# Softmax denominators from one product per head: GpSimd adds the node blocks first, and the product moves behind the value sums

## The chip, the cores and the metric

The kernel runs on one core of a Trainium2 chip. The metric is the device time of one execution in microseconds (us); lower is better. Each kernel was run several times, and times are medians of these runs. All runs told here were of the fast state; the verdict on a change is "faster" or "slower" only beyond 2%. Ratios are computed as the mean time of one kernel's fast runs over that of the other's fast runs of the same rounds, which is not quite the ratio of the medians quoted.

In profile lines PE is TensorE (PEld its weight loads), DVE is VectorE, ACT is ScalarE, POOL is GpSimd, and L722 is line 722 of the kernel.

## The reference, cut to what matters

Two layers on 64 graphs of 256 nodes: a graph-attention layer with a feed-forward block, then an attention layer with 8 heads of 32 features whose values depend on the adjacency (0 or 1 here).

```python
scores = jnp.einsum('bhid,bhjd->bhij', q, k) / np.sqrt(dh)
attn = jax.nn.softmax(scores, axis=-1)
for r in range(Wv.shape[0]):
    v_r = (src @ Wv[r] + bv[r]).reshape(Bb, Nn, h, dh).transpose(0, 2, 1, 3)
    mask = (adj_matrix == r)[:, None]
    out = out + jnp.einsum('bhij,bhjd->bhid', attn * mask, v_r)
```

The kernel works with the transposed exponentials e[j, i] (nodes j on the 128 partitions, so two node blocks). The denominator of row i is a sum over all j, that is over partitions and over both blocks; TensorE forms it as a product with a block of ones.

## The kernel before

A turn of the main loop takes the attention of one pair of graphs together with the first layer's stages of two later pairs, so that TensorE always has something to do. There are 32 turns with attention. A turn has four quads: two graphs, each with two groups of four heads. In what follows "step" is the time from one turn to the next, "the last step" the one from the last turn but one to the last, and "the tail" the time from the last turn's first value product (vp) to the end.

```python
def weighted(u, b, m, q, k_, aT):               # scores, exponentials, masked product
    ps = [bank(f"sp{n}_{a}") for a in range(HPB)]
    ...                                          # sp: scores of four heads
    e = work.tile([P, HPB, NB * N], F32, tag="e", name=f"e{n}")
    ea = work.tile([P, HPB, NB * N], F32, tag="ea", name=f"ea{n}")
    for a in range(HPB):
        nc.scalar.activation(e[:, a, :], ps[a], AF.Exp, scale=isd)
    for a in range(0, HPB, 2):                   # two instructions, two heads each
        nc.vector.tensor_tensor(ea[:, a:a + 2, :], e[:, a:a + 2, :],
                                ab[:, None, :].to_broadcast([P, 2, NB * N]), ALU.mult)
    return e, ea

def applied(b, m, v, e, ea, po, zo):             # zo: denominators, po: value sums
    terms = [(zo, lambda h, j: ones, e), (po, ..., e), (po, ..., ea)]
    ...                                          # per term: two node blocks x four heads

def divided(u, b, po, zo, oT):
    nc.vector.reciprocal(rz, zo)
    nc.gpsimd.tensor_add(low, low, rz)
    nc.vector.tensor_tensor(oT[...], po..., rz..., ALU.mult)

def normed(u, l, y):                             # layer norm; rs is on GpSimd
    ...
    nc.gpsimd.tensor_tensor(rs, ve, mhalf, ALU.pow)
    ...

def affine(u, l, xn, g, b):                      # res, L644 and L645
    nc.gpsimd.tensor_mul(r, xn, g...)
    nc.gpsimd.tensor_add(r, r, b...)

# in a turn, TensorE runs in this order (cut):
hT = to_features(Y["y"], ...)                    # h2T
second_sums(x_)                                  # ygp; then yg = normed(...), affine(...)
q, k_ = queries_keys(y_, hT)
h1hT = to_features(X["y"], ...)                  # h1T: transposes of yg
v = values(y_, hT)                               # vp
e = {0: weighted(y_, *quads[0], q, k_, aT)}
h1 = hidden(...)                                 # h1p, first half
e[1] = weighted(y_, *quads[1], q, k_, aT)
apply_(0)
e[2] = weighted(y_, *quads[2], q, k_, aT)
apply_(1)
e[3] = weighted(y_, *quads[3], q, k_, aT)
hidden(...)                                      # h1p, second half
early(z)                                         # transposes of a later pair
apply_(2)
apply_(3)
...
res = affine(y_, 3, yn, rg4, rb4)                # last thing of the turn, then the store
```

zo and po have one PSUM bank each. TensorE's order is the program's; the other engines are ordered by the framework's scheduler.

## Time and profile before

| | before |
|---|---|
| time (median of 3 runs) | 3486.24 us |
| TensorE busy | 97% of the span |
| one turn | 105.80 us |
| zo in a turn | 64 instructions (4 quads of 16) |
| GpSimd busy | 28% |

TensorE is the engine to look at: a turn is as long as TensorE takes for it, plus the waits of TensorE. The prediction shows the busy shares, the chain in order of time and the timelines on which it rests. Two groups by line (columns: busy us, mean ns of one instruction, idle time before them):

```profile
L710 DVE TENSOR_TENSOR ea<-e,aT 128x1024 f32<-128x1024 f32 x256 | 317.9, 1283 | 272.7 <-ACT e L708 272.7
L722 PE MATMUL zo<-e,ones 128*32 128x256 f32 x2048 | 137.1, 385 | 3.0 <-DVE rz L728 3.0
```

And TensorE's timeline at the start of a turn:

```profile
1822.05 3.60 PE L674 MATMUL kp<-h2T,wk 128*128 128x512 f32 x8
1827.04 1.65 PE L540 MATMUL h1T17p<-ident,yg 128*128 128x128 f32 x8 [1.39 <-DVE yg L637]
```

TensorE waits 1.39 us for yg and then takes 1.65 in place of 1.04 us for the eight transposes, because yg comes in four pieces: VectorE's four instructions for it begin 0.32 us apart (1826.48 to 1827.45), and the second to fourth transposes begin 0.23 to 0.32 apart (1827.04 to 1827.91), the last three 0.11.

### The profile page before, as it was taken

Reading aid. Unit: us, or ns where it says so; the run is one execution under the profiler, and the core shown is the slowest. Engines: PE = TensorE matmul, PEld = TensorE weight load, DVE = VectorE, ACT = ScalarE, POOL = GpSimd, SP = SyncE. Lnnn points to the kernel's source line nnn. Section 1 sums busy time; section 2 is a strip of 40 time slices with the busy share of each in tenths; the row PEclk is TensorE's granted clock in tenths of the full one; section 3 lists DMA queues with packets and bytes.
Section 4 is the critical chain, followed back from the end, with each engine's and each line's share of the span. In section 5 each row is a group of like instructions: output and inputs, shape, how many; then the busy total and the mean of one; then the engine's idle time right before and its main releaser. Section 6 shows DMA issues by size and latency. Waiting matters only on the chain.

```text
span 3486.0 us, 45212 instructions
## 1 busy us (share of the span) xinstructions
PE 3368.1 (97%) x18970; PEld 2201.8 (63%) x18970; DVE 1688.8 (48%) x3479; ACT 1080.4 (31%) x1920; POOL 984.6 (28%) x844
## 2 busy tenths in 40 slices
PE   5899999999999999999999999999999999999997
PEld 3566666666665666665666666666656665656664
DVE  2545455445454444554454554454544445544544
ACT  1323333323323323333333333233233233333322
POOL 1233232332222332322332323322223323223312
PEclk7999999999999999999999999999999999999998
DMA  4000000000000000000000000000000000000000
GB/s 119 19 13 19 7 19 19 13 19 10 16 19 19 13 19 7 19 19 19 13 19 7 19 19 13 19 12 14 19 19 13 19 7 19 19 19 7 7 1 14
DMA packets 62465, 61.04 MB, mean 18 GB/s; under 512 B 7216, under 2 KB 61616, under 8 KB 62256
## 3 DMA queue, kind: packets, MB, share of 16 engines
q1 hardware_dynamic: 33792, 33.56, 3.0%
q0 software_dynamic: 16896, 16.78, 2.1%
q10 hardware_dynamic: 11568, 7.76, 0.8%
q8 instruction: 151, 2.47, 0.3%
q14 instruction: 58, 0.48, 0.0%
HBM read 41.31 MB, written 16.78 MB: 17 GB/s over the span
## 4 chain that ended last, share of the span: by engine, by line
PE 86%; POOL 6%; DVE 6%; issue 1%; ACTq 1%; DMA 0%; ACT 0%; POOLq 0%; DVEq 0%
PE h1p L655 26%; PE yfp L617 25%; PE vp L686 6%; PE po L722 6%; PE sp L702 4%; PE zo L722 4%; PE hpp L606 3%; PE yop L617 3%; PE xpp L568 3%; POOL res L644 2%; POOL res L645 2%; POOL rs L633 2%; DVE yf L637 1%; DVE h2T L544 1%; PE rows L578 1%
## 5 line engine op out<-in xcount | busy, mean ns | idle before, releaser
L655 PE MATMUL h1p<-h1T,wf 128*128 128x512 f32 x1024 | 458.1, 600 | 0.1
L710 DVE TENSOR_TENSOR ea<-e,aT 128x1024 f32<-128x1024 f32 x256 | 317.9, 1283 | 272.7 <-ACT e L708 272.7
L655 PE MATMUL h1p<-h3T,w 128*128 128x512 f32 x1024 | 446.7, 594 | 1.4 <-DVE h3T L544 1.4
L617 PE MATMUL yfp<-wf,h 128*128 128x256 f32 x2048 | 447.3, 379 | 0.0
L617 PE MATMUL yfp<-w,h 128*128 128x256 f32 x2048 | 447.3, 379 | 0.0
L617 PEld LDWEIGHTS yfp<-w,h 128*128 128x128 f32 x2048 | 386.8, 190 | 52.2 <-issue 1.0
L617 PEld LDWEIGHTS yfp<-wf,h 128*128 128x128 f32 x2048 | 386.7, 190 | 51.3
L708 ACT ACTIVATE e<-sp 128x512 f32<-128x512 f32 x512 | 264.3, 603 | 444.9 <-PE sp L702 444.9
L655 PEld LDWEIGHTS h1p<-h3T,w 128*128 128x128 f32 x1024 | 195.0, 191 | 234.4 <-issue 229.5
L729 POOL TENSOR_TENSOR low<-low,rz 128x512 f32<-128x512 f32 x64 | 81.2, 1269 | 917.2 <-DVE rz L728 917.2
L655 PEld LDWEIGHTS h1p<-h1T,wf 128*128 128x128 f32 x1024 | 190.1, 190 | 236.9 <-issue 218.2
L587 DVE SCALAR_TENSOR_TENSOR s<-s 128x512 f32<-128x512 f32 x128 | 90.2, 706 | 443.3 <-ACT s L584 442.0
L645 POOL TENSOR_TENSOR res<-res,rb 128x1024 f32<-128x1024 f32 x128 | 301.3, 2354 | 10.0
L620 DVE TENSOR_TENSOR yf<-yfp,res 128x512 f32<-128x512 f32 x128 | 88.5, 692 | 424.6 <-PE yfp L617 423.4
L633 POOL TENSOR_TENSOR rs<-ve,mhalf 128x4 f32<-128x4 f32 x128 | 130.7, 1021 | 457.9 <-DVE ve L632 457.9
L657 ACT ACTIVATE h<-h1p,b 128x512 f32<-128x512 f32 x256 | 175.9, 687 | 251.1 <-PE h1p L655 249.8
L728 DVE RECIPROCAL rz<-zo 128x512 f32<-128x512 f32 x64 | 214.7, 3354 | 67.8 <-PE zo L722 67.8
L657 ACT ACTIVATE h<-h1p,bf 128x512 f32<-128x512 f32 x256 | 177.1, 692 | 216.0 <-PE h1p L655 216.0
L686 PE MATMUL vp<-wv,h2T 128*128 128x512 f32 x512 | 225.0, 592 | 0.0
L676 ACT ACTIVATE q<-qp,bq 128x512 f32<-128x512 f32 x64 | 44.0, 688 | 530.8 <-PE qp L674 530.8
L608 ACT COPY hp<-hpp 128x258 f32<-128x258 f32 x128 | 48.0, 375 | 442.0 <-PE hpp L606 442.0
L644 POOL TENSOR_TENSOR res<-yf,rg 128x1024 f32<-128x1024 f32 x64 | 150.8, 2356 | 95.8 <-DVE yf L637 94.3
(485 smaller groups left out, 4343.4 us busy)
## 6 DMA issues: line engine op xcount, KB each, us to landing
xs<-in_x_dram SPq DMA_DIRECT2D x32, 512.0 KB, 3.8
af<-in_adj_dram POOLq DMA_DIRECT2D x32, 512.0 KB, 4.5
out_dram<-res SPq DMA_DIRECT2D x32, 512.0 KB, 2.9
wf<-in_L_gnn_w_ff_dram ACTq DMA_DIRECT2D x2, 1024.0 KB, 11.4
w<-in_L_gnn_W_dram ACTq DMA_DIRECT2D x2, 1024.0 KB, 9.5
wv<-in_L_gnn_Wv_dram ACTq DMA_DIRECT2D x2, 256.0 KB, 4.5
gw<-in_L_gnn_W_dram ACTq DMA_DIRECT2D x1, 256.0 KB, 4.5
gw2e<-in_L_gnn_W_dram ACTq DMA_DIRECT2D x1, 256.0 KB, 6.9
```

The source lines that it names most:

```text
L617: nc.tensor.matmul(ps[:, i * F:(i + 1) * F], lhs(t, k), rhs(b, k), start=(k == 0), stop=(k == n - 1))
L633: nc.gpsimd.tensor_tensor(rs, ve, mhalf, ALU.pow)
L644: nc.gpsimd.tensor_mul(r, xn, g[:, None, :].to_broadcast([P, T, F]))
L645: nc.gpsimd.tensor_add(r, r, b[:, None, :].to_broadcast([P, T, F]))
L655: nc.tensor.matmul(ps, wi[:, k, f * P:(f + 1) * P], hT[:, k, :], start=(k == 0), stop=(k == KB - 1))
L657: nc.scalar.activation(h1[:, f, :], ps, func, bias=bi[:, f:f + 1])
L686: nc.tensor.matmul(ps, hT[:, k, t * P:(t + 1) * P], wvf[:, k, :], start=(k == 0), stop=(k == KB - 1))
L702: nc.tensor.matmul(ps[a][:, j * N:(j + 1) * N], k_[hp, m, j0:j0 + P], q[hp, m, b * N:(b + 1) * N], start=True, stop=True)
L708: nc.scalar.activation(e[:, a, :], ps[a], AF.Exp, scale=isd)
L710: nc.vector.tensor_tensor(ea[:, a:a + 2, :], e[:, a:a + 2, :], ab[:, None, :].to_broadcast([P, 2, NB * N]), ALU.mult)
L722: nc.tensor.matmul(to[hp, m * N:(m + 1) * N], lhs(m * HPB + a, j), rhs[:, a, j * N:(j + 1) * N], start=(n < 2 and j == 0), stop=(n != 1 an ...
L728: nc.vector.reciprocal(rz, zo)
```

## The change

The intent: TensorE is the bound, and half of the products with ones can go if the two node blocks of e are added first. The add goes to GpSimd, which is idle 72% of the time, and zo goes behind po to give the add time.

```diff
-        return e, ea
+        es = work.tile([P, HPB, N], F32, tag="es", name=f"es{n}")
+        nc.gpsimd.tensor_add(es, e[:, :, 0:N], e[:, :, N:2 * N])
+        return e, ea, es
...
-        terms = [(zo, lambda h, j: ones, e), (po, ..., e), (po, ..., ea)]
...
+        terms = [(j, v[:, b * NB + j, r * F + m * P:r * F + (m + 1) * P], w)
+                 for r, w in ((0, e), (1, ea)) for j in range(NB)]
+        for n, (j, vs, w) in enumerate(terms):
+            for a in range(HPB):
+                hp = slice(a * DH, (a + 1) * DH)
+                nc.tensor.matmul(po[hp, m * N:(m + 1) * N], vs[:, hp], w[:, a, j * N:(j + 1) * N],
+                                 start=(n == 0), stop=(n == len(terms) - 1))
+        for a in range(HPB):
+            nc.tensor.matmul(zo[a * DH:(a + 1) * DH, m * N:(m + 1) * N], ones, es[:, a, :],
+                             start=True, stop=True)
```

More of the change, by code (lines that the diff above doesn't have):

```diff
@@ L711, in weighted, with applied @@
                                     ab[:, None, :].to_broadcast([P, 2, NB * N]), ALU.mult)
-        return e, ea
-    def applied(b, m, v, e, ea, po, zo):
-        terms = [(zo, lambda h, j: ones, e), (po, lambda h, j: v[:, b * NB + j, h * DH:(h + 1) * DH], e),
-                 (po, lambda h, j: v[:, b * NB + j, F + h * DH:F + (h + 1) * DH], ea)]
-        for n, (to, lhs, rhs) in enumerate(terms):
-            for j in range(NB):
-                for a in range(HPB):
-                    hp = slice(a * DH, (a + 1) * DH)
-                    nc.tensor.matmul(to[hp, m * N:(m + 1) * N], lhs(m * HPB + a, j),
-                                     rhs[:, a, j * N:(j + 1) * N],
-                                     start=(n < 2 and j == 0), stop=(n != 1 and j == NB - 1))
+        es = work.tile([P, HPB, N], F32, tag="es", name=f"es{n}")
+        nc.gpsimd.tensor_add(es, e[:, :, 0:N], e[:, :, N:2 * N])
+        return e, ea, es
+    def applied(b, m, v, e, ea, es, po, zo):
+        terms = [(j, v[:, b * NB + j, r * F + m * P:r * F + (m + 1) * P], w)
[8 more added lines that the diff above has]
+                             start=True, stop=True)
     def divided(u, b, po, zo, oT):
```

## The prediction

> **What bounds the kernel now.** I read the page first: busy shares, then the chain that ended last.
>
> ```profile
> PE 3368.1 (97%) x18970; PEld 2201.8 (63%) x18970; DVE 1688.8 (48%) x3479; ACT 1080.4 (31%) x1920; POOL 984.6 (28%) x844
> ...
> PE 86%; POOL 6%; DVE 6%; issue 1%; ACTq 1%; DMA 0%; ACT 0%; POOLq 0%; DVEq 0%
> ```
>
> TensorE has work 97% of the span and carries 86% of the chain, so a product taken away there is time won unless something makes TensorE wait. The busy figure alone does not say what a product costs, because the matmuls overlap: the table of groups gives 379 ns for one, though many run at once. For spacing I read the chain in order of time, in one turn of the loop (columns: start us, length us, what). There are 32 such turns, 105.80 us apart (the pieces of the chain from 1708.69 and from 1814.49 begin alike).
>
> ```profile
> 1843.69 1.08 PE sp L702 x16
> 1844.77 1.00 PE zo L722 x16
> 1845.77 1.73 PE po L722 x32
> 1847.49 1.08 PE sp L702 x16
> 1848.57 1.00 PE zo L722 x16
> 1849.57 1.73 PE po L722 x32
> 1851.30 1.08 PE sp L702 x16
> 1852.37 7.06 PE h1p L655 x16
> 1859.43 0.87 PE aTp L555 x8
> 1860.31 0.87 PE xT18p L540 x8
> 1861.18 1.00 PE zo L722 x16
> 1862.18 1.73 PE po L722 x32
> 1863.91 0.86 PE zo L722 x16
> 1864.77 1.73 PE po L722 x32
> 1866.50 1.92 PE yop L617 x8
> ```
>
> No gap anywhere: here TensorE sets the pace. One quad is sp (scores), zo (denominators, 16 instructions), po (value sums, 32). po runs at 1.73/32 = 54 ns an instruction, and so does the zo that follows a po (0.86/16). A zo that follows other work takes 1.00, so changing over to the column tiles costs 0.14. The scores run one quad ahead: sp at 1843.69 is quad 1's, the zo and po after it are quad 0's. Quad 1's scores end at 1844.77 and its zo starts at 1848.57, the shortest way from scores to use; quads 0, 2 and 3 have h1p (7.06 us) and more in between.
>
> What runs beside quad 1 and after, from the timeline of ScalarE, VectorE and GpSimd:
>
> ```profile
> 1844.78 2.07 ACT L708 ACTIVATE e<-sp 128x512 f32<-128x512 f32 x4 [0.37 <-PE sp L702]
> ...
> 1845.90 2.36 DVE L710 TENSOR_TENSOR ea<-e,aT 128x1024 f32<-128x1024 f32 x2 [5.78 <-ACT e L708]
> ...
> 1856.04 2.85 DVE L710 TENSOR_TENSOR ea<-e,aT 128x1024 f32<-128x1024 f32 x2
> ...
> 1855.41 1.27 POOL L729 TENSOR_TENSOR low<-low,rz 128x512 f32<-128x512 f32 x1 [22.69 <-DVE rz L728]
> ```
>
> The exponentials of quad 1 end at 1846.85, its two masked products ea at 1848.26. GpSimd is idle from 1832.7 to 1855.41. The ea pair of quad 3 takes 2.85 in place of 2.36: it began inside GpSimd's low, which ended at 1856.68.
>
> [...] the 0.49 lost above. It recurs: ea's mean is 1283 ns and its median 1221, and 256 x 0.062 = 16 us is 0.5 in each of 32 turns. It also shows who goes next, in an early turn:
>
> ```profile
> 114.70 1.83 DVE L587 SCALAR_TENSOR_TENSOR s<-s 128x512 f32<-128x512 f32 x1
> 116.45 2.83 DVE L587 SCALAR_TENSOR_TENSOR s<-s 128x512 f32<-128x512 f32 x1
> ...
> 113.63 2.35 POOL L644 TENSOR_TENSOR res<-yf,rg 128x1024 f32<-128x1024 f32 x1 [1.50 <-DVE yf L637]
> 116.06 2.67 POOL L645 TENSOR_TENSOR res<-res,rb 128x1024 f32<-128x1024 f32 x1
> ```
>
> L587 normally takes 0.71 (its group's mean). The first waits out L644 (ends 115.98); L645, waiting from 116.06, then gets in ahead of the second, though VectorE issued the two back to back; the second ends at 119.28, 0.55 after L645. [...]
> [...] an untiled product of the same 256 columns costs 447.3/2048 = 218 ns (group yfp of the page), four column tiles share that time at 54 ns each; and the changeover is the 0.14.
> [...] Here: 2354 ns (L645) against 1221 for the usual ea, both 128x1024, 1.93 times.
>
> **The change, part by part.**
> Removed: per quad, two ones-products per head become one: 8 of 16 zo instructions. 8 x 54 ns = 0.43 us; 128 quads (4 in each of 32 turns): 55.4 us. The changeover of 0.14 stays and moves to po. All of it lies on TensorE's unbroken stretch.
> Added: per quad one GpSimd add, 128x1024 out, two inputs; by L645's row 2.35 us. 128 x 2.35 = 301 us of GpSimd, which goes from 985 to about 1286 us (37%): no bound. Taken beside TensorE, if in time.
> Moved: zo goes behind po, so the reciprocal starts later against the end of the quad. For the second graph: zo end, reciprocal 3.35, then (the built order puts the addition yo in between) 0.65 and oT 0.69, together 4.75; until its user, the second yop, TensorE has the first yop 1.92 and xpp 3.51 = 5.43. It fits by about 0.7. For the first graph h1p and the transposes lie between, 8.8 us.
>
> Now whether es is in time, quad by quad. Quad 0 has h1p between scores and use: in time. Quads 2 and 3: [...] (es 2.35, ea 1.2 each, reciprocal, low 1.27) I get ea and es of quad 3 done 0.6 to 1.3 us before their use. Quad 1 is the tight one. In the new order, from sp at 1843.69: po of quad 0 starts 1844.77, 1.87 long, zo 0.43, sp of quad 2 1.08, so po of quad 1 starts at 1848.15: its e half to 1849.15, the first ea instructions to about 1849.37, po's end 1850.02, then zo.
> es of quad 1 can start at 1846.9 (exponentials ended 1846.85). The first ea ends at 1847.12, the second starts right behind. As in the early turn, I expect [...] es to end at 1849.4, and the second ea, 1.08 after that (1857.76 against 1856.68 in quad 3; the earlier pair's 0.55 is for half the size), at 1850.45. TensorE, which needs the second ea at 1849.37, waits 1.1 us a turn: 32 x 1.1 = 35 us.
> Sum: 3486.2 - 55.4 + 35 = 3466.
>
> **The rivals.**
> (A) The sum above: [...] 3466. For it: the alternation shown. Against: GpSimd would be ahead by some 0.1 us only.
> (B) [...] ea is on time (1848.26), es runs 1848.2 to 1850.55, and zo, due at 1850.02, waits 0.55: 32 x 0.55 = 18 us, 3449. For it: VectorE's second product is issued before the first ends.
> (C) No collision that matters: 3486.2 - 55.4 = 3431. For it: es alone would end at 1849.3, 0.7 before its use. Against: the 0.49 of quad 3, turn after turn.
> (D) GpSimd lateness spreads: low, the load of adj or the second oT come later and TensorE stops at yop or xpp as well, another 0.5 us a turn on top of A: 3482. Slacks of 0.6 to 1.3 speak against it.
> GpSimd as the bound of the whole (37%) is out.
>
> **Range and chances.** I give A 0.52, B 0.27, C 0.15, D 0.06. Mean: 0.52 x 3466 + 0.27 x 3449 + 0.15 x 3431 + 0.06 x 3482 = 3457; I state 3458, between A and B. Range from C to a bad A: 3431 to 3476. Faster by over 2% is below 3416.5; even the full 55 us is only 1.6%, so 0.03. Slower by over 2% (3556) would need over 3.9 us of new waits a turn: 0.01.
>
> **What would show it.** zo's instructions fall from 2048 to 1024 and its group's busy time to about half of 137 us; ea's mean rises above 1283 ns, with one of quad 1's two at about 3.4 us; in the chain, a VectorE piece between the po instructions of quad 1 (A), a GpSimd piece between po and zo (B), or neither (C). The step of 105.80 us a turn should become about 105.2 (A), 104.6 (B) or 104.1 (C). I am wrong if an instruction saved is worth other than 54 ns, if the wait in quad 1 is not there or much longer, or if TensorE waits in a quad that I called safe.

Cut from this text, where marked, are passages on the hardware that no trace of this case shows. The sum came to 3466: 3486.2 - 55.4 (saved) + 35 (32 waits of 1.1 us). The 1.1 is the estimate, from lengths in the traces: es ends at 1849.4 if it goes in behind the first ea (2.35 us, L645's row), and the second ea 1.08 after it, as in quad 3. That es goes in there is taken from one early turn alone, in which L645 began at 116.06 and the second L587 at 116.45. The 0.6 to 1.3 us for quads 2 and 3 are an estimate as well, with the lengths given there laid one after the other over both engines. In rival A the add goes ahead of the second ea, in rival B behind it. The "changeover" is the measured difference of 1.00 and 0.86 us: in the single records the first four zo behind the scores begin 0.32 us after the last four of these (1844.37 and 1844.70) and the next four 0.24 later, in place of 0.22 each. What TensorE does in it was not shown.

## The result, and the profile after

The changed kernel took 3495.82 us (3495.09 to 3496.76, 6 runs) against 3485.89 us before: ratio 1.0029, 95% interval 1.0016 to 1.0042. It is 10 us slower, within 2%, and above the stated range of 3431 to 3476.

The page's busy shares and chain, and the groups that answer to those shown of before:

```profile
PE 3333.4 (95%) x17946; PEld 2172.3 (62%) x17946; DVE 1950.5 (56%) x3479; ACT 1083.9 (31%) x1920; POOL 1358.4 (39%) x972
...
PE 82%; DVE 10%; POOL 6%; issue 1%; ACTq 1%; DMA 0%; ACT 0%; POOLq 0%
...
L710 DVE TENSOR_TENSOR ea<-e,aT 128x1024 f32<-128x1024 f32 x256 | 527.5, 2101 | 162.5 <-ACT e L708 162.5
L713 POOL TENSOR_TENSOR es<-e 128x1024 f32<-128x1024 f32 x128 | 347.5, 2715 | 414.9 <-ACT e L708 414.9
```

The 1024 zo instructions are gone from TensorE (18970 to 17946). VectorE gained 262 us of busy time though it got no new instruction: the mean ea went from 1283 to 2101 ns. VectorE's share of the chain went from 6% to 10%. Now one turn's chain in order of time (start, length, what); it starts, like the one in the prediction, at the scores of quad 1:

```profile
1839.25 1.08 PE sp L702 x16
1840.33 1.17 PE po L723 x17
1841.50 0.02 issue
1841.52 1.02 DVE ea L710
1842.54 0.13 issue
1842.67 3.46 DVE ea L710
1846.12 0.04 issue
1846.17 0.84 PE po L723 x10
1847.01 0.01 PE zo L726 x2
1847.02 0.20 PE po L723 x2
1847.22 0.43 PE zo L726 x6
1847.65 1.08 PE sp L702 x16
```

A second ea of 3.46 us stands between two stretches of po. GpSimd's add, and TensorE at the same place:

```profile
1842.55 2.48 POOL L713 TENSOR_TENSOR es<-e 128x1024 f32<-128x1024 f32 x1 [5.65 <-ACT e L708]
...
1844.52 0.60 PE L723 MATMUL po<-ea,v 128*32 128x256 f32 x4
1846.17 0.84 PE L723 MATMUL po<-ea,v 128*32 128x256 f32 x10 [1.04 <-DVE ea L710]
```

The add starts at 1842.55, 0.12 before the second ea, and ends at 1845.03; that ea ends at 1846.11. At its usual pace TensorE would be done with the four ea instructions of the first line at 1844.52 + 4 x 0.054 = 1844.74; it goes on at 1846.17, 1.43 later (the line's 1.04 counts from the modelled end of the fourth). In the single records po begins four at a time, the four within 0.02 us, and the next four 0.216 us (4 x 0.054) later. The first ea holds only two of the four heads, so these four instructions began two at a time, at 1844.52 and 1844.74, and took two such slots and not one: of the 1.43, TensorE stood still for 1.21 (1846.17 - 1844.74 - 0.216). From the scores of quad 1 to those of quad 3 it takes 1847.65 - 1839.25 = 8.40 us, against 1851.30 - 1843.69 = 7.61 before. Two quads should have saved 0.86, so the wait cost 8.40 - (7.61 - 0.86) = 1.65. Quads 2 and 3 save their 0.86 undisturbed. The turn is thus about 0.1 shorter than before: the trace has 105.70 for 105.79 (measured from the first vp of one turn to that of the next), so that of the saving of 1.73 the wait takes 1.64.

The whole difference of the two traces, by stretches of TensorE's timeline:

| stretch | before | after | difference |
|---|---|---|---|
| start to the first vp | 135.85 | 132.78 | -3.07 |
| 30 steps from turn to turn | 3173.78 | 3172.94 | -0.84 |
| last step | 93.54 | 95.58 | +2.04 |
| last turn's vp to the end | 82.80 | 92.27 | +9.47 |
| span | 3485.97 | 3493.58 | +7.60 |

The first row varies between 131.3 and 136.6 over the fourteen experiments below without regard to their edits, so it is no effect of the change. The 30 steps would be -2.6 but for two steps of 106.11 and 106.99 among the 105.70s, together +1.7. The last two rows are where the loss is: in the last turns no later pair fills TensorE's time. TensorE's timeline there, before:

```profile
3424.18 1.94 PE L722 MATMUL zo<-e,ones 128*32 128x256 f32 x16 [3.02 <-DVE rz L728]
...
3433.74 1.99 PE L617 MATMUL yop<-wo,oT 128*128 128x256 f32 x8 [0.64 <-DVE oT L730]
```

and after:

```profile
3416.49 0.84 PE L723 MATMUL po<-ea,v 128*32 128x256 f32 x10 [2.06 <-DVE ea L710]
...
3431.36 1.94 PE L723 MATMUL po<-e,v 128*32 128x256 f32 x16 [7.36 <-DVE oT L733]
...
3441.95 1.99 PE L617 MATMUL yop<-wo,oT 128*128 128x256 f32 x8 [2.69 <-DVE oT L733]
```

Before, the second graph's zo came first and waited 3.02 us for the reciprocal of the first graph (one bank). Now its po comes first and waits 7.36 us for oT, which comes after that reciprocal, which in turn started only when zo, behind po, was done. The add has a part in it too: po of the last turn's quad 0, which has no h1p before it there, waits 2.06 us for ea. By the view by windows TensorE is busy 59.94 us of this tail and was busy 59.83 of it before, so the 9.47 us are all waiting.

### The profile page after: what moved, and what is told of

Read it like the earlier page. It is cut to its first block, busy times and chain, and to the rows that moved or that the text cites. A ratio compares the mean times of both kernels' runs of the same rounds, so it can differ in the third digit from the quotient of the medians.

```text
span 3493.6 us, 43357 instructions
## 1 busy us (share of the span) xinstructions
PE 3333.4 (95%) x17946; PEld 2172.3 (62%) x17946; DVE 1950.5 (56%) x3479; ACT 1083.9 (31%) x1920; POOL 1358.4 (39%) x972
## 4 chain that ended last, share of the span: by engine, by line
PE 82%; DVE 10%; POOL 6%; issue 1%; ACTq 1%; DMA 0%; ACT 0%; POOLq 0%
PE h1p L655 26%; PE yfp L617 25%; PE vp L686 6%; PE po L723 5%; DVE ea L710 4%; PE hpp L606 3%; PE yop L617 3%; PE xpp L568 3%; PE sp L702 3%; POOL res L644 2%; POOL res L645 2%; POOL rs L633 2%; PE zo L726 1%; DVE yf L637 1%; DVE h2T L544 1%
## 5 line engine op out<-in xcount | busy, mean ns | idle before, releaser
L710 DVE TENSOR_TENSOR ea<-e,aT 128x1024 f32<-128x1024 f32 x256 | 527.5, 2101 | 162.5 <-ACT e L708 162.5
L713 POOL TENSOR_TENSOR es<-e 128x1024 f32<-128x1024 f32 x128 | 347.5, 2715 | 414.9 <-ACT e L708 414.9
L587 DVE SCALAR_TENSOR_TENSOR s<-s 128x512 f32<-128x512 f32 x128 | 90.2, 706 | 443.3 <-ACT s L584 441.9
L645 POOL TENSOR_TENSOR res<-res,rb 128x1024 f32<-128x1024 f32 x128 | 301.3, 2354 | 10.0
L732 POOL TENSOR_TENSOR low<-low,rz 128x512 f32<-128x512 f32 x64 | 108.8, 1699 | 301.6 <-DVE rz L731 301.6
```

The source lines that it names most:

```text
L645: nc.gpsimd.tensor_add(r, r, b[:, None, :].to_broadcast([P, T, F]))
L713: nc.gpsimd.tensor_add(es, e[:, :, 0:N], e[:, :, N:2 * N])
```

## The experiments

Theory L: the add goes in between the two ea of quad 1 (in the changed kernel 0.12 us ahead of the second, which then took 3.46 us in place of 1.22), TensorE waits for the second, and the order costs at the end. Passages of the expectations that told more of the hardware than the traces show are cut where marked. In all experiments the turns are measured from the trace as above. The runs of the kernel before, beside them, had medians of 3486.02 to 3486.81.

### Batch 1: the parts alone

**e1_no_add**: one product, fed with the first node block alone, no add (wrong result, relative error 0.24).

```diff
-        es = work.tile([P, HPB, N], F32, tag="es", name=f"es{n}")
-        nc.gpsimd.tensor_add(es, e[:, :, 0:N], e[:, :, N:2 * N])
...
-            nc.tensor.matmul(zo[...], ones, es[:, a, :],
+            nc.tensor.matmul(zo[...], ones, e[:, a, 0:N],
```

> One product with ones per quad, fed with the first node block alone; no add at all (the result is wrong on purpose). Theory L [...]: without the add only the saving of 128 x 0.43 = 55 us is left, 3431 to 3438 us, and no wait of po on ea. Rival O (zo behind po makes reciprocal and oT late, and TensorE waits there): as slow as the changed kernel, 3490 or more. Rival W (the saving per product is smaller than 54 ns an instruction): between 3445 and 3486 without any new wait.

Measured: 3468.51 us, ratio 0.9947 (0.9930 to 0.9963). No wait of po on ea is left, yet only 18 us of the 55 came. The steps between turns are of two kinds: 104.06 us, which is 105.79 less the predicted 1.73, in 13 turns; and 105.67 to 105.76 in 16 (one is 104.50). Two turns of each kind, as the view by windows shows them (columns: window, its length, TensorE busy, granted clock, DMA share, GB/s):

```profile
1190.80:1296.56 105.76, 104.39 (x563) 0.98 0.06 16
1296.56:1402.32 105.76, 104.39 (x563) 0.98 0.05 16
2243.27:2347.33 104.06, 102.68 (x562) 1.00 0.06 16
2347.33:2451.39 104.06, 102.69 (x562) 1.00 0.05 16
```

The same instructions, but the granted clock is 0.98 in the long turns. The trace's clock records show why: in each long turn the clock is at half for one stretch of 3.41 us, during vp, which then takes 1.70 us longer (8.66 for 6.96); everything else in the turn is equal to 0.02 us. The half stretch follows the wait before h1T. In each of the seven traces counted further below, the half stretches begin on a grid of 3.4133 us, to within 1 ns. So none of my three theories held whole: L had the saving right, but a cause that nobody had named took most of it back (16 x 1.70 = 27 us; the last step and the tail took another 2.1 + 5.3). I call it theory C: the idle time before h1T brings on the half stretch, and with it the 1.70 us.

**e2_order_only**: two products as before, behind po, no add.

```diff
-        for a in range(HPB):
-            nc.tensor.matmul(zo[...], ones, es[:, a, :], start=True, stop=True)
+        for j in range(NB):
+            for a in range(HPB):
+                nc.tensor.matmul(zo[...], ones, e[:, a, j * N:(j + 1) * N],
+                                 start=(j == 0), stop=(j == NB - 1))
```

> The kernel before with its two ones-products per head moved behind po; no add. Theory L: the order alone costs nothing in the steady turns and 2 to 5 us in the last turn, where no other work lies between: 3486 to 3492 us. Rival O: the order costs the missing 65 us, about 3550.

Measured: 3495.09 us, ratio 1.0023 (1.0006 to 1.0039). All 30 steps are 105.79, as before; the last step is 95.67 (+2.1) and the tail 90.53 (+7.7). The order alone costs about 9 us, all at the end: as a steady cost rival O is out, and as a cost at the end it is twice what I had written. The waits themselves are only 5.5 of these 9.8 us. The rest is the clock again, which the trace shows at half after the longer wait in the tail:

```profile
3427.99 1.94 PE L721 MATMUL po<-e,v 128*32 128x256 f32 x16 [4.78 <-DVE oT L732]
3429.67 1.96 PE L721 MATMUL po<-ea,v 128*32 128x256 f32 x16
3431.38 1.96 PE L725 MATMUL zo<-e,ones 128*32 128x256 f32 x16
...
3434.34 1.05 PE L721 MATMUL po<-ea,v 128*32 128x256 f32 x16
```

Sixteen instructions take 1.96 us there in place of 1.05. By the view by windows TensorE is busy 64.17 us of this tail, against 59.83 before with the same 395 instructions: 4.3 us for the clock.

**e3_add_only**: the kernel before, with the add computed and unused.

```diff
+        es = work.tile([P, HPB, N], F32, tag="es", name=f"es{n}")
+        nc.gpsimd.tensor_add(es, e[:, :, 0:N], e[:, :, N:2 * N])
         return e, ea
```

> The kernel before with the GpSimd adds in place but their result unused. Theory L: [...] the zo that still stands before po (16 instructions, 1.0 us) leaves TensorE at that point just as it comes: 0 to 0.3 us a turn, 3486 to 3496. Rival: the add costs its time wherever it stands [...]: about 3550, as the changed kernel would be without its saving.

("It" is the second ea of quad 1, which took 3.46 us in the changed kernel; about 3.4 were expected here.)

Measured: 3516.21 us, ratio 1.0082 (1.0066 to 1.0099), above what I expected. The common step is 106.15 (+0.36: with zo in front, TensorE needs ea later, and most of the delay is hidden). But six of the 30 steps are 107.84, 1.7 longer again: the halved clock. 30 x 0.36 + 6 x 1.7 = 21; the last step (+0.9) and the tail (+8.1: longer waits, such as 5.6 us for the reciprocal in place of 3.0, and 3.2 us more of TensorE's busy time for the same instructions, at a halved clock) bring it to 30. ea's mean was 2394 ns. So the add does harm by itself, though not its full length per quad.

**e4_vector_add**: the change with the add on VectorE.

```diff
-        nc.gpsimd.tensor_add(es, e[:, :, 0:N], e[:, :, N:2 * N])
+        nc.vector.tensor_add(es, e[:, :, 0:N], e[:, :, N:2 * N])
```

> The change with the add on VectorE, behind the two masked products of each quad (1.22 us each). Theory L: [...] the second masked product of quad 1 on time and the sum 1.2 us after it, 0.4 to 0.5 us before zo needs it: 3431 to 3440 us. Rival O: no gain against the changed kernel, 3490 or more. Rival V (VectorE, now 128 x 1.22 = 156 us busier, becomes late for the copies of xT or for oT): 3445 to 3470 with waits at xpp or yop.

Measured: 3473.96 us, ratio 0.9965 (0.9948 to 0.9982). Ten steps are within 0.01 of 104.06, the others up to 105.76, again with half stretches of the clock. ea's mean is back at 1274 ns, no wait of po on ea is among TensorE's longest waits, and the clock takes its part as in e1.

### Batch 2: the add beside ea and the clock, each by itself

**e6_memset**: GpSimd only writes es (wrong, relative error 0.50).

```diff
-        nc.gpsimd.tensor_add(es, e[:, :, 0:N], e[:, :, N:2 * N])
+        nc.gpsimd.memset(es, 1.0)
```

> The change with GpSimd only writing es (a constant; the result is wrong on purpose) in place of adding two inputs. Theory L [...]: ea as fast as before (1.2 us each), no wait of po on ea, and turns of 104.06 us wherever the clock is not halved, as without any add; with the halved windows that the run without an add showed, 3465 to 3475 us. Rival [...]: the second ea of quad 1 about 3.4 us and turns of 105.7, about 3495.

("Halved windows", here and in e9, are half stretches of 3.41 us as in e1.)

Measured: 3467.09 us, ratio 0.9944 (0.9927 to 0.9960). ea's mean is 1273 ns, no wait on ea, free turns of 104.07; turns with a halved clock as in e1 (the profiled execution was the slowest of the four, 3476.07). The memset need not wait for e, but in the trace 64 of the 256 ea have a whole memset of 0.95 us inside them and still take 1.22 us: this memset, which reads nothing, did not hold ea up.

**e9_fill**: e1 with useless products in TensorE's idle time before h1T.

```diff
             q, k_ = queries_keys(y_, hT)
+            if have(x_):
+                fill = bank(f"fill{y_}")
+                for n in (TN, TN // 2):
+                    nc.tensor.matmul(fill[:, :n], wq[:, 0, 0:P], hT[:, 0, 0:n], start=True, stop=True)
```

> The kernel without the add (e1), with two useless products (1.29 us) put into TensorE's idle time before h1T. Theory C [...]: no halved window between the first and the last turn, all turns 104.06 us; 3438 to 3445 us, 25 to 30 less than e1 although it does more work. Rival (the 105.7 us turns of e1 have another cause[...]): still some 17 turns of 105.7, 3468 or more.

Measured: 3441.65 us, ratio 0.9870 (0.9853 to 0.9886), in the stated range. All 30 steps are 104.05 to 104.08. 124 more TensorE instructions of useless work made the kernel 27 us faster than e1. The transposes behind the filled gap still took 1.64 us, so here it was the idle time itself that mattered, and not the slowly fed transposes alone.

**f2_late_affine**: the kernel before with the turn's last affine and store moved into the next turn, behind the normalisation of yg.

```diff
-            res = affine(y_, 3, yn, rg4, rb4)
-            nc.sync.dma_start(out[...], res)
+            last.append((y_, yn))
...
         if have(x_):
             second_sums(x_)
+        if last:
+            put()          # the affine and the store of the turn before
```

> The kernel before with one thing moved: the last affine of a turn and its store come after the next turn's normalisation on GpSimd, so that rs, and with it yg and h1T, no longer wait behind it. The idle 1.39 us and the 0.78 us of the slowly fed transposes should go: turns of 103.6 us in place of 105.8, 3415 to 3425 us. Rival: the idle time is only moved, to rs or to the next user of GpSimd: 3470 to 3490.

Measured: 3422.75 us, ratio 0.9818 (0.9802 to 0.9835). All steps are 103.64. TensorE before h1T, and GpSimd:

```profile
1165.66 3.60 PE L674 MATMUL kp<-h2T,wk 128*128 128x512 f32 x8
1169.09 1.04 PE L540 MATMUL h1T11p<-ident,yg 128*128 128x128 f32 x8
...
1166.41 1.01 POOL L633 TENSOR_TENSOR rs<-ve,mhalf 128x4 f32<-128x4 f32 x1 [3.63 <-DVE ve L632]
1168.92 2.35 POOL L644 TENSOR_TENSOR res<-yg,rg 128x1024 f32<-128x1024 f32 x1 [1.50 <-DVE yg L637]
```

rs no longer stands behind two instructions of 2.35 us, the idle time is gone, and the transposes take 1.04 again.

**f4_change_late**: the change on top of it.

> The change itself on top of the late affine[...]. Theory L plus last turn: turns within 0.2 us of the late affine's own (saving 1.73, wait 1.64), and 8 to 12 us more at the end: 3423 to 3437, slower than the late affine alone. Rival (the change fails only by the clock): 1.7 us less a turn than the late affine, about 3370.

Measured: 3436.02 us, ratio 0.9854 (0.9838 to 0.9870). Steps of 103.58 for 103.64, last step +3.7, tail +12.5. With no halved clock in the 30 steps, the change is still 13 us slower than f2: the wait in quad 1 (33.4 us in 32 waits of po on ea, by the view of waits) gives nearly the whole saving back, and the end, where the clock is at half in places again, costs the rest.

### Batch 3: the order of add and ea, and the remedies

**g1_held** and **g2_held_zo_later**, both on f4:

```diff
+        hold = work.tile([P, 1], F32, tag="hold", name=f"hold{n}")
+        nc.gpsimd.tensor_copy(hold, ea[:, HPB - 1, NB * N - 1:])
         nc.gpsimd.tensor_add(es, e[:, :, 0:N], e[:, :, N:2 * N])
# g2 only: zo of quad 1 is issued after the scores of quad 3
-            apply_(1)
+            after = apply_(1)
             e[3] = weighted(y_, *quads[3], q, k_, aT)
+            after()
```

> The change on the late affine, with GpSimd made to read one column of the second ea before each add[...] (rival B of the prediction, made to happen). Theory L: both ea of quad 1 at 1.2 us, the add 0.2 us after them, and TensorE waits 0.8 to 1.0 us before zo in place of 1.64 within po: turns of 102.7 to 102.9 us (103.64 - 1.73 + 0.9) against 103.58 with the add unheld; 3406 to 3418 us. Rival (the order of the two does not matter[...]): 103.5 or more a turn.

> As the held one, and the zo of quad 1 put behind the scores of quad 3 (1.08 us more for the add). Theory L: no wait left in quad 1; one changeover of the tiles more (0.14 to 0.25): turns of 102.0 to 102.2 us, 3384 to 3396 us. Rival: the wait stays, over 102.6 a turn.

(The 0.14 is the prediction's 1.00 - 0.86; in the changed kernel's chain the 17 po behind scores take 1.17 us, 0.25 over 17 x 0.054.)

Measured: 3434.05 us with steps of 103.58, and 3444.34 us with 103.71 (ratios 0.9852 and 0.9883). Neither tested what it should: the copy had no tie to the add, and the scheduler put it behind. The traces show es first and the copy after ea, so nothing was held. By accident g2 shows that moving zo alone is no help (+0.13) as long as the wait is on ea.

**g3_held_again** and **g4_held_zo_later_again**: the copy writes into es, so the add must follow it.

```diff
-        hold = work.tile([P, 1], F32, tag="hold", name=f"hold{n}")
-        nc.gpsimd.tensor_copy(hold, ea[:, HPB - 1, NB * N - 1:])
+        nc.gpsimd.tensor_copy(es[:, 0, 0:1], ea[:, HPB - 1, NB * N - 1:])
```

> The held add, now truly held: the one column of the second ea is copied into es, which the add then overwrites. Theory L: both ea of quad 1 at 1.2 us; the add ends about 7.25 us after the start of quad 1's scores, zo is due at 6.3: a wait of 1.0 before zo and none in po, turns of 102.8 to 103.1 us against 103.58 unheld; 3412 to 3424 us. Rival (order does not matter): 103.5 or more a turn.

> The held add, and the zo of quad 1 behind the scores of quad 3, where it is due at 7.4 us. Theory L: no wait in quad 1 or one under 0.2 us; turns of 102.0 to 102.3 us (101.91 and the 0.13 that the moved zo cost in g2_held_zo_later); 3386 to 3400 us. Rival: over 102.8 a turn.

Measured for g3: 3427.41 us, ratio 0.9829 (0.9813 to 0.9845), steps of 103.32. The group of zo shows where TensorE waits now:

```profile
L727 PE MATMUL zo<-es,ones 128*32 128x256 f32 x1024 | 80.5, 386 | 40.5 <-POOL es L714 40.5
```

Both ea of quad 1 took 1.22 us and po ran through; TensorE waits 40.5 us in all before zo, in place of the 33.4 in po in f4. Holding the add back moved the wait, as theory L says, but gained only 103.58 - 103.32 = 0.26 a turn, less than the 0.5 to 0.8 that I had written, as the copy's start and length put 0.4 us between ea and add. Measured for g4: 3396.18 us, ratio 0.9740 (0.9723 to 0.9756), steps of 102.25, as expected: with the add held and zo due 1.08 us later, the wait is gone (0.34 above f1's 101.91 are left; the moved zo cost 0.13 in g2, the rest was not traced). So, by these two runs and f4, what cost was that two ea and the add, one after the other in either order, took 1.2 + 2.4 + 1.2 us, more than quad 1 had between its exponentials and their use. Who was first decided only which product waited (po 33.4 us in f4, zo 40.5 in g3).

**f1_vector_late**: the add on VectorE (e4) with the late affine.

> Both remedies: the add on VectorE and the late affine. Theory: the saving in full in every turn and no halved clock, turns of 101.9 us (103.64 - 1.73), 3375 to 3386 us, faster than the kernel before by about 3%. Rival (VectorE now late for rs, yg or h1T): waits of TensorE before h1T again, 102.5 us or more a turn.

Measured: 3379.28 us, ratio 0.9693 (0.9679 to 0.9706). All steps are 101.91, that is 103.64 - 1.73 to the digit.

**f3_vector_late_end**: f1 with the old order and two products in the last two turns.

```diff
+        if u >= NG - 2:
+            return e, ea, None
...
+        if es is None:
+            for j in range(NB):
+                for a in range(HPB):
+                    nc.tensor.matmul(zo[...], ones, e[:, a, j * N:(j + 1) * N],
+                                     start=(j == 0), stop=(j == NB - 1))
```

> As the last, with the denominators of the last two turns by the old order (two products, zo ahead of po, no add), since zo behind po delays reciprocal and oT where no work of later turns fills the time. Theory E (the order costs 8 to 12 us at the end): 8 to 12 us less than the kernel with both remedies, 3365 to 3376 us; last step between turns back to about 93.5 and tail to about 82.5. Rival (the end was long for another cause): the same as that kernel within 2 us.

Measured: 3369.17 us, ratio 0.9663 (0.9650 to 0.9676). The last step is 93.53 and the tail 82.80, both as before, and the gain over f1 is 10 us: the order's cost at the end, found a second time, again with the halved clock in it (TensorE busy 59.82 us of the tail, in f1 62.29 with 32 instructions fewer). This kernel is correct and beats both the kernel before (by 3.4%) and the changed one.

## Why the prediction was wrong, point by point

**The bound and the saving** were right. TensorE sets the pace, and eight instructions at 54 ns a quad are 1.73 us a turn: 105.79 to 104.06 (e1, e9), 103.64 to 101.91 (f1).

**The mechanism in quad 1** was right, size off. Rival A happened: the add began 0.12 us ahead of the second ea, that ea ended 1.08 us after it, and TensorE waited inside po (34.0 us in 32 waits of po on ea by the view of waits, the last of them in another quad). The term "32 x 1.1 = 35 us" was mis-sized: it measured 1.64 a turn, which over 32 turns is 52 us. Three things make the difference. TensorE got to the second ea 0.19 earlier than I had it (in the frame of the prediction 1849.18, not 1849.37), because I took the bounds of the chain's pieces for start times: before, the chain has quad 1's po at 1849.57, where the timeline has its first instruction at 1849.39. The add itself took 2.48 us in place of 2.35 (its record begins 0.20 before the first ea ends at 1842.75), so the second ended 0.1 later. These make 1.43 of idle time. The last 0.21 (1.64 - 1.43) comes after the wait: the 20 instructions that were left took 1847.65 - 1846.17 = 1.48 us, where 20 x 0.054 = 1.08 and the usual 0.14 make 1.22. The single instructions of the trace show why: the two heads of the first ea had run ahead, so the 20 began in six slots of 0.216 us and not five, the last two slots (1847.05 and 1847.27) with two instructions in place of four. Slot by slot the cost is 1.21 of standing still and two extra slots of 0.216, one before and one after the wait: 1.64.

**"It fits by about 0.7"**, the part of the reasoning on zo behind po, failed. (Its 4.75 is 0.06 more than the three terms that it names, 4.69; that changes nothing.) It was checked in turns that have a later pair's work between. The last two turns have none, and there the order costs 2.1 + 7.7 us (e2, and f3 gives 10 back): 5.5 us of longer waits for the late reciprocal and what hangs on it, and 4.3 of halved clock after them. In the changed kernel itself these two turns lost 2.0 + 9.5 us, with waits for ea (1.0 and 2.06 us) among them.

**Rival C's 3431** was out of reach, which the prediction could not know from one turn's chain: without any collision e1 took 3468. Before, a turn of 105.79 us is close to 31 steps of the grid of 3.4133 us on which the half stretches begin (105.81), so TensorE's one idle time fell at nearly the same place in the grid, turn after turn, and at that place no half stretch followed it (none in the 30 steps). A turn of 104.06 moves it. The seven traces that still have the idle time (before, after, e1, e2, e3, e4, e6) have 30 such waits each in the loop, 1.36 to 1.57 us long: 59 of the 210 began 0.07 to 1.02 us after a point of the grid, and all 59 were followed by a halved stretch; 146 began 1.09 to 3.37 after, and none was; the other five lie on the edge. Once hit, a turn takes 104.06 + 1.70 = 105.76, again nearly 31 steps of the grid, so the place comes back only 0.06 us earlier each time and it takes about 1.0/0.06 = 17 turns to get out: e1 has 16 long turns in a row and a part of one before them. That the place in the grid is the cause is an inference from these counts, and what sets the clock was not shown; that the idle time is, e9 and f2 show by removing it. In the changed kernel itself this cost only two steps, 1.7 us (one half stretch of 3.41 us, from 2246.51).

**The sum.** 3486.2 - 51.9 (saving in the 30 steps) + 49.2 (their waits in quad 1) + 11.5 (last step and tail, all in) + 1.7 (clock) = 3496.7; measured 3495.8. So of the 30 us that the 3466 missed, about 16 lie in the size of quad 1's wait, 13 in the last two turns and 2 in the clock.

**The checks** that I named: zo's instructions fell to 1024, as said; its busy time to 92.2 us and not to half of 137, because a group's busy time counts the last matmul of each stretch at its whole 379 ns and not at 54, so this check was badly chosen. GpSimd's busy time became 1358 and not 1286 us, as its instructions got longer too (the add's mean is 2715 ns, in place of L645's 2354). Quads 0, 2 and 3 were safe, as said, but for quad 0 of the last turn (2.06 us).

## What to carry to other kernels

Before giving work to an idle GpSimd, look at what VectorE does in the same microseconds: here ea, with two inputs in SBUF, took 3.46 us beside an add that reads SBUF, in place of 1.22, and 1.22 beside a memset. Lay the two end to end and see who needs the result first; here the same add on VectorE was free (f1: 101.91 us a turn, the whole 1.73 saved). Check a change of order also in the turns that have no later work to hide behind. And take out TensorE's short regular idle times before tuning anything else in a loop: here a turn of 104.06 us in place of 105.79 moved one of 1.4 us to where a half stretch of the clock followed it, and the saving of 1.73 us a turn showed as 0.03 to 0.12 in 16 turns of e1.
